# Layer norm inside a window attention's pipeline, weights on GpSimd, and an output stage by whole samples

## The chip, the cores and the metric

The kernel runs on one core of a Trainium2 chip, in one launch. The time is device microseconds of that core, the median of several runs; lower is better. Engines: PE multiplies matrices (PEld is its weight load), DVE is VectorE, ACT is ScalarE, POOL is GpSimd; SP issues most of the DMAs.

## What is computed

The input x has 4 samples of 56 x 56 tokens with 128 channels, float32. Four layers follow each other, each `x = x + layer(group_norm(x))`:

```python
# layer 0: attention in shifted 7x7 windows, then over all tokens, then an MLP
attn_wins = _mha(wins, wq, bq, wk, bk, wv, bv, wo, bo)
xf = xf + _mha(_layernorm(xf, g1, be1), wq, bq, wk, bk, wv, bv, wo, bo)
h = gelu(_layernorm(xf, g2, be2) @ w1 + b1)
xf = xf + (h @ w2 + b2)
# layer 1: edge layer, relu over all pairs of a row, summed
# layer 2: attention whose queries, keys, values and projection are
#   products in the Fourier domain, over the 56 images of a sample
scores = einsum('bhtd,bhsd->bhts', qs, ks) / sqrt(d)
out = einsum('bhts,bhsd->bhtd', softmax(scores), vs)
attention = inorm(fourier(out, wP) + xa)
m = gelu(inorm(fourier(inorm(attention), wM0)) + skip)
m = inorm(fourier(m, wM1)) + skip
output = inorm(m) + attention
# layer 3: convolution over 3 rows, with sums over both axes
g = (agent_sum + time_sum - y) / scale
out = relu(g + res)
```

`inorm` normalizes each image; the group norm has 32 groups of 4 channels.

## The kernel before, in words

Channels lie on the 128 partitions, and a sample is 128 x 3136. Layers 0 and 1 run sample by sample: `fast_windows` (L294), `fast_attention` (L492), the MLP and the edge layer, with about 716 us from one sample to the next. Then come the Fourier layer's stages for all samples together, and last the output stage.

`fast_windows` takes 8 groups of 8 windows (392 tokens). Its loop at the function's end has 12 turns; in each turn a stage of its own works on another group: norm, project, score, value, turn, output. PE, ACT and DVE run in the order in which the code names the instructions (`manual_schedule`); elsewhere a scheduler chooses the order, and then only the engines named in `manual_schedule` keep the code's. The PSUM tag `mm` has four banks.

`fast_attention` begins with a loop over 7 blocks of 448 tokens. In each, PE centres the block (L631), ACT squares it (L633), PE forms the variance (L641), ACT takes the root (L643), DVE the reciprocal (L644), and DVE multiplies the centred block, which lies in PSUM, by it (L520). Two blocks later PE forms queries and keys (L526) and values (L535); ACT moves them out (L527, L537). The normed tokens lie in the ring that later holds the exponentials (L602 writes it, L555 sums it).

The spectra of layer 2 run after the last sample (2910 to 3043 us), `s_pr` being one of their transforms. After them `value_weights` (L1277) loads V, Vrev and P, and DVE makes from them the weights that `attend` loads as `dd`. `attention_weights` (L1334) calls `score_weights` (L1311) on DVE, and then multiplies spectra by these weights: q_u by DVE at L1402, by POOL at L1399, with a product on PE at L1389. `attend` (L1446) uses the result, and `attended_rows` (L1519) turns it into rows and writes them to `yd` in DRAM.

The output stage works on half samples of 28 images. `outputs` (L1958) starts one every 7 turns; in each turn every living half sample does one of its 28 steps, and after the second half of a sample `last_layer` (L1870) follows with its own. All four compute engines keep this written order. A half sample loads a (`xm`) and y (`yd`), and goes back from the Fourier domain with `over_h` (L1665, on PE, seven products with the data as weights) and `over_c` (L1676); ACT scales in between (L1684). It sums squares on PE (L1724) after ACT squared (L1735 takes the root, L1730 adds up). `over_w` (L1692) goes into the Fourier domain, `weighted` (L1707) goes on along the other axis, DVE multiplies by the layer's weights (L1711) and POOL adds the two parts (L1716). This happens for the projection's image, for M0 and for M1. POOL and DVE add images (L1809 to L1861), and DVE takes statistics (L1864), row sums (L1865) and column sums (L1866). `last_layer` folds the group norm into the convolution's weights (`wr`), so that x needs no pass of its own, and the convolution reads x (L1941).

Of the kernel before, what the change touches and what calls it, by code (L numbers as in the profile page):

```python
# [11 lines left out]
F32 = mybir.dt.float32  # L12
# [281 lines left out]
def fast_windows(k, w, xw, xf, mr):  # L294
# [11 lines left out]
    BUFS = 3  # L306
    with ExitStack() as es:
# [20 lines left out]
        scores, values, outs, columns = {}, {}, {}, {}  # L328

        def bank():  # L330
            return psum.tile([P, 512], F32, tag="mm", name="w_mm", bufs=4)
# [65 lines left out]

        norm(0)
        norm(1)
        for n in range(NG + 4):  # L400
            for stage, g in ((norm, n + 2), (project, n), (score, n - 1), (value, n - 2), (turn, n - 3), (output, n - 4)):
                if 0 <= g < NG:
                    stage(g)
# [88 lines left out]
def fast_attention(k, w, xf):  # L492
# [9 lines left out]
    with ExitStack() as es:  # L502
# [3 lines left out]
        va = big.tile([P, 25, P], F32, name="f_va")  # L506

        ring = big.tile([P, RING, NB], F32, name="f_ring")
        h1 = ring[:, 0:NBLK, :].rearrange("p a n -> p (a n)")
        with tc.tile_pool(name="f_ln", bufs=2) as lk, tc.tile_pool(name="f_ps0", bufs=2, space=PSUM) as psum, \  # L510
                tc.manual_schedule(engines={mybir.EngineType.PE}):
            centred, var = {}, {}
            c0 = 0
            for j in range(NBLK + 2):
                if j < NBLK:
                    centred[j] = psum.tile([P, 512], F32, tag="c", name="f_pc")
                    centre(k, lk, centred[j][:, :NB], xf[:, blk(j)], var, j)
                if 0 < j <= NBLK:
                    r = inverse_deviation(k, lk, psum, var.pop(j - 1))
                    nc.vector.tensor_mul(h1[:, blk(j - 1)], centred.pop(j - 1)[:, :NB], r)  # L520
                if j < 2:
                    continue
                b = blk(j - 2)
                for dst, wt, bias in ((qT, w.fq, w.fbq), (kT, w.fk, w.fbk)):
                    pm = psum.tile([P, 512], F32, tag="mm", name="f_pq", bufs=4)
                    nc.tensor.matmul(pm[:, :NB], wt, h1[:, b], start=True, stop=True)  # L526
                    nc.scalar.activation(dst[:, b], pm[:, :NB], AF.Identity, bias=bias)  # L527

                while c0 < 25 and min(c0 * P + 4 * P, TOK) <= b.stop:
                    pm = psum.tile([P, 512], F32, tag="mm", name="f_pv", bufs=4)  # L530
                    n = min(4, 25 - c0)
                    for i in range(n):
                        c = c0 + i
                        for o in half if c == 24 else (slice(0, P),):
                            nc.tensor.matmul(pm[o, i * P:(i + 1) * P], h1[:, c * P:min(c * P + P, TOK)], w.fv,  # L535
                                             start=True, stop=True)
                    nc.scalar.copy(va[:, c0:c0 + n, :].rearrange("p a c -> p (a c)"), pm[:, :n * P])  # L537
                    c0 += 4
        wk = es.enter_context(tc.tile_pool(name="f_wk", bufs=2))
        ps = es.enter_context(tc.tile_pool(name="f_ps", bufs=1, space=PSUM))  # L540
        oT = big.tile([P, TOK], F32, name="f_oT")
# [440 lines left out]
def l2_constants():  # L982
# [44 lines left out]
    c["gw"] = np.concatenate([np.stack([ck * np.cos(a), -ck * np.sin(a)], 1)] * 4)  # L1027
    c["gv"] = np.concatenate([np.stack([ck ** 0.5 * np.cos(a), -ck ** 0.5 * np.sin(a)], 1)] * 4)
# [99 lines left out]
def normed_images(k, w, st, b, pools, x2d, xad, ready):  # L1128
# [16 lines left out]
    nc.gpsimd.memset(xp[:, HH, :], 0.0)  # L1145
# [131 lines left out]
def value_weights(k, I, w, dd):  # L1277


    nc, tc = k.nc, k.tc  # L1280
    with ExitStack() as es:
        wk = es.enter_context(tc.tile_pool(name="d_wk", bufs=1))
        load_weights(k, wk, I, "w2_", w, ("V", "Vrev", "P"))

        half = wk.tile([32, 2, HH], F32, name="d_half")
        nc.vector.tensor_add(half[:, 0, :], w.V[0:32, 0, 0, :], w.Vrev[:, 0, :])
        nc.vector.tensor_sub(half[:, 1, :], w.V[0:32, 1, 0, :], w.Vrev[:, 1, :])
        nc.vector.tensor_scalar_mul(w.V[0:32, :, 0, :], half, 0.5)
        m = wk.tile([P, 8, HH], F32, name="d_m")
        nc.vector.tensor_scalar_add(m, w.V[:, 0], w.pvh[:, 1:2])  # L1290
        d = wk.tile([P, 2, 8, HH], F32, name="d_d")
        t = wk.tile([P, 8, HH], F32, name="d_t")
        nc.vector.tensor_mul(d[:, 0], w.P[:, 0], m)
        nc.vector.tensor_mul(t, w.P[:, 1], w.V[:, 1])
        nc.vector.tensor_sub(d[:, 0], d[:, 0], t)
        nc.vector.tensor_mul(d[:, 1], w.P[:, 1], m)
        t2 = wk.tile([P, 8, HH], F32, name="d_t2")
        nc.vector.tensor_mul(t2, w.P[:, 0], w.V[:, 1])
        nc.vector.tensor_add(d[:, 1], d[:, 1], t2)
        f = wk.tile([P, 3, 8, HH], F32, name="d_f")  # L1300
        for ri in range(2):
            flat = d[:, ri].rearrange("p c r -> p (c r)")
            nc.vector.scalar_tensor_tensor(flat, w.V[:, ri].rearrange("p c r -> p (c r)"), w.pvh[:, 0:1], flat,
                                           ALU.mult, ALU.add)
        nc.scalar.copy(f[:, 0], d[:, 0])
        nc.vector.tensor_sub(f[:, 1], d[:, 1], d[:, 0])
        nc.vector.tensor_add(f[:, 2], d[:, 0], d[:, 1])
        nc.sync.dma_start(dd.rearrange("n g h i x -> (g h i) n x"), f.rearrange("p n c r -> p n (c r)"))


def score_weights(nc, pool, qk, qkr, qks, m, out):  # L1311

    for x in range(2):
        col0 = qk[:, x, :, 0, :]
        nc.vector.tensor_add(col0[:, 0], col0[:, 0], qkr[:, x, 0])
        nc.vector.tensor_sub(col0[:, 1], col0[:, 1], qkr[:, x, 1])
        if x:
            nc.vector.tensor_scalar_mul(col0, col0, m[:, 3:4])  # L1320
        nc.vector.scalar_tensor_tensor(col0[:, 0], qks[:, x], m[:, 2 * x:2 * x + 1], col0[:, 0], ALU.mult, ALU.add)
        if qk.shape[3] > 1:
            s = pool.tile([P, HEADS], F32, tag="s", name="q_skip")
            nc.vector.tensor_scalar_mul(s, qks[:, x], m[:, 1:2])
            rest = qk[:, x, 0, 1:, :]
            nc.vector.tensor_add(rest, rest, bc(s, 1, rest.shape[1]))
    t = pool.tile([P] + list(out.shape[2:]), F32, tag="t", name="q_t")
    for n, (i, op) in enumerate(((1, ALU.add), (0, ALU.subtract))):
        nc.vector.tensor_mul(out[:, n], qk[:, 0, 0], qk[:, 1, n])
        nc.vector.tensor_mul(t, qk[:, 0, 1], qk[:, 1, i])  # L1330
        nc.vector.tensor_tensor(out[:, n], out[:, n], t, op)


def attention_weights(k, I, w, st):  # L1334
# [5 lines left out]
    nc, tc = k.nc, k.tc  # L1340
    with ExitStack() as es:
# [250 lines left out]
CONV_WEIGHTS = ("M0", "M0rev", "M1", "M1rev", "ms", "nb")  # L1592


def conv_weights(k, w, pool, late):

# [527 lines left out]
```

## Time and profile before

| What | us |
|---|---|
| median of 3 runs | 4117.6 |
| lowest and highest run | 4115.57 and 4118.82 |
| profiled execution, its time | 4115.57 |
| profiled execution, its span | 4113.8 |
| windows of sample 1 | 50.7 to 104.5 |
| layer norm and projections of sample 1 | 104.5 to 154.8 |
| spectra of layer 2 | 2910 to 3043 |
| output stage | 3606 to 4114 |

The span runs from the first to the last instruction of the profiled execution; its time has 1.8 us around it. The mean clock granted to PE was 0.929 of full speed. A busy share is a mean over a stretch, and says nothing of what ends a wait. In a row of instructions the mean time of one follows the busy time; "PE n <- ACT m: 20, 7, 5" reads: PE waited 20 us in 7 waits for ACT's m, the longest 5.

### The profile page before, as it was taken

Reading aid. Unit: us, or ns where it says so; the run is one execution under the profiler, and the core shown is the slowest. Engines: PE = TensorE matmul, PEld = TensorE weight load, DVE = VectorE, ACT = ScalarE, POOL = GpSimd, SP = SyncE. Lnnn points to the kernel's source line nnn. Section 1 sums busy time; section 2 is a strip of 40 time slices with the busy share of each in tenths; the row PEclk is TensorE's granted clock in tenths of the full one; section 3 lists DMA queues with packets and bytes.
Section 4 is the critical chain, followed back from the end, with each engine's and each line's share of the span. In section 5 each row is a group of like instructions: output and inputs, shape, how many; then the busy total and the mean of one; then the engine's idle time right before and its main releaser. Section 6 shows DMA issues by size and latency. Waiting matters only on the chain. (4 is left out here: it accounts for less than half of the span.)

```text
span 4113.8 us, 79308 instructions
## 1 busy us (share of the span) xinstructions
PE 3593.8 (87%) x35320; PEld 1623.8 (39%) x35320; DVE 2930.3 (71%) x2659; ACT 2097.6 (51%) x2214; POOL 1145.9 (28%) x596
## 2 busy tenths in 40 slices
PE   6899989989998988999898899989769799877877
PEld 4322234532223453222355322245543333355554
DVE  6688859668885967888586788858658577625443
ACT  4677745567773546777454777745210122133331
POOL 0000018300001820000272000027116489724554
PEclk9999989999998999999899999989779899967777
DMA  2000000000000000000000000000210488330100
GB/s 90 1 1 1 1 16 3 18 1 1 1 1 16 3 18 1 1 1 1 16 3 17 1 1 1 1 1 3 100 65 1 94 174 166 85 110 24 55 16 32
DMA packets 75001, 117.55 MB, mean 29 GB/s; under 512 B 62300, under 2 KB 64092, under 8 KB 69404
## 3 DMA queue, kind: packets, MB, share of 16 engines
q1 hardware_dynamic: 15964, 99.55, 8.1%
q10 hardware_dynamic: 58688, 12.85, 1.9%
q8 instruction: 279, 4.57, 0.5%
q14 instruction: 70, 0.57, 0.0%
HBM read 82.67 MB, written 29.72 MB: 27 GB/s over the span
## 5 line engine op out<-in xcount | busy, mean ns | idle before, releaser
L602 ACT ACTIVATE f_ring<-f_s 128x1792 f32<-128x1792 f32 (+3 forms) x796 | 1098.0, 1430 | 312.8 <-PE f_s L600 310.9
L555 DVE TENSOR_TENSOR f_acc<-f_acc,f_ring 128x1792 f32<-128x1792 f32 x560 | 1134.1, 2025 | 81.8 <-ACT f_ring L602 26.4
L600 PE MATMUL f_s<-f_qT,f_kT 32*128 32x448 f32 x5376 | 738.7, 571 | 56.9 <-ACT f_ring L602 24.1
L844 POOL TENSOR_TENSOR x<-xf,xw 128x343 f32<-128x343 f32 (+2 forms) x36 | 30.0, 834 | 2142.2 <-issue 2069.9
L561 PE MATMUL f_po<-f_ring,f_va 128*32 128x448 f32 x5376 | 589.7, 546 | 0.0
L928 DVE TENSOR_TENSOR e_td<-e_pa,e_c 128x1792 f32<-128x1792 f32 x252 | 491.4, 2016 | 8.0 <-ACT e_a L895 8.0
L930 POOL TENSOR_TENSOR e_tp<-e_a,e_c 128x1792 f32<-128x1792 f32 x140 | 451.7, 3260 | 143.6 <-PE e_acc L935 104.5
L600 PEld LDWEIGHTS f_s<-f_qT,f_kT 32*128 32x128 f32 x5376 | 267.4, 183 | 536.7 <-ACT f_ring L602 366.1
L935 PE MATMUL e_acc<-e_td,t_shared 32*32 32x448 f32 x8064 | 322.2, 545 | 25.9 <-DVE e_td L928 15.3
L932 ACT ACTIVATE e_tp<-e_tp 128x1792 f32<-128x1792 f32 x140 | 235.2, 1697 | 187.3 <-POOL e_tp L930 187.3
L1496 DVE TENSOR_TENSOR u_ud<-u_px,u_d 112x1792 f32<-112x1792 f32 x144 | 240.2, 1708 | 104.6 <-PE u_po L1501 85.9
L561 PEld LDWEIGHTS f_po<-f_ring,f_va 128*32 128x32 f32 x5376 | 132.8, 108 | 398.3 <-issue 397.3
L644 DVE RECIPROCAL n_r<-n_r 128x392 f32<-128x392 f32 (+1 forms) x60 | 163.6, 2749 | 110.3 <-ACT n_r L643 110.1
L1501 PE MATMUL u_po<-u_ud,AT 112*64 112x448 f32 x960 | 202.2, 551 | 35.2 <-DVE u_ud L1496 35.2
L935 PE MATMUL e_acc<-e_tp,t_shared 32*32 32x448 f32 x4480 | 220.4, 544 | 2.4 <-ACT e_tp L932 2.2
L1498 POOL TENSOR_TENSOR u_up<-xh,u_d 112x1792 f32<-112x1792 f32 x64 | 195.2, 3075 | 33.5 <-PE u_po L1501 17.6
L935 PEld LDWEIGHTS e_acc<-e_td,t_shared 32*32 32x32 f32 x8064 | 133.4, 103 | 150.5 <-DVE e_td L928 60.5
L555 DVE TENSOR_TENSOR f_acc<-f_ring 128x1792 f32<-128x1792 f32 x28 | 56.7, 2025 | 115.4 <-ACT f_ring L602 115.4
L1389 PE MATMUL q_acc<-q_u,S 64*64 64x448 f32 x1024 | 104.4, 559 | 30.2 <-DVE q_u L1402 25.4
L1501 PEld LDWEIGHTS u_po<-u_ud,AT 112*64 112x64 f32 x960 | 65.2, 138 | 160.4 <-issue 87.4
L1501 PE MATMUL u_po<-u_up,AT 112*64 112x448 f32 x576 | 126.7, 547 | 0.0
L935 PEld LDWEIGHTS e_acc<-e_tp,t_shared 32*32 32x32 f32 x4480 | 94.1, 103 | 54.6 <-ACT e_tp L932 18.5
(452 smaller groups left out, 4756.8 us busy)
## 6 DMA issues: line engine op xcount, KB each, us to landing
u_d<-dd SPq DMA_DIRECT2D x48, 784.0 KB
xw<-in_x SPq DMA_DIRECT2D x4, 1568.0 KB
x2d<-x SPq DMA_DIRECT2D x4, 1568.0 KB
x_xs<-xad ACTq DMA_DIRECT2D x32, 196.0 KB
xm<-x_ev ACTq DMA_DIRECT2D x64, 98.0 KB
o_a<-xm SPq DMA_DIRECT2D x8, 784.0 KB
o_x<-x2d SPq DMA_DIRECT2D x4, 1568.0 KB
out<-o_o SPq DMA_DIRECT2D x12, 448.0 KB
```

The source lines that it names most:

```text
L555: nc.vector.tensor_add(acc, slots(j, 0) if c == 1 else acc, slots(j, c))
L561: nc.tensor.matmul(po[heads[h], :NB], va[o, c, heads[h]], p, start=(c == 0), stop=(c == 24))
L600: nc.tensor.matmul(ss[:, i, :NB], kT[heads[h], c * P:(c + 1) * P], qT[heads[h], blk(j)], start=True, stop=True)
L602: nc.scalar.activation(ring[:, slot:slot + m, :], ss[:, :m, :NB], AF.Exp, scale=scale)
L644: nc.vector.reciprocal(r, r)
L928: nc.vector.tensor_tensor(t, am, cm, ALU.max)
L930: nc.gpsimd.tensor_sub(t, bc(a.rearrange("p (l n) -> p l n", l=8), 1, 4), cm)
L932: nc.scalar.activation(tf, tf, AF.Relu)
L935: nc.tensor.matmul(acc[quarters[q], r, :NB], k.ident[o, o], t[o, q].rearrange("p l n -> p (l n)"), start=(g == 0), stop=(g == len(EDGE_TUR ...
L1496: nc.vector.tensor_mul(u, bc(px[:, :, :NB], 2, m), dm)
L1498: nc.gpsimd.tensor_mul(u, bc(x, 2, m), dm)
L1501: nc.tensor.matmul(po[64 * b2:64 * b2 + 64, :NB], st.AT[:, 8 * i + h0 + q, 2 * bp + b2, :], u[:, b2, q, :], start=(left == 16), stop=(left ...
```

## The change

Three parts change at once.

1. `fast_windows` is called from `fast_attention` and gets the tiles for queries, keys and values. Four stages join its loop: `central` five groups behind the newest, `variance` six, `divide` ten and `attended` eleven, so that the loop has 19 turns. The blocks are the windows' groups of 392. Four groups share one variance bank, 32 partitions each, and so one root and one reciprocal; `divide` spreads the reciprocal over the partitions by a product on PE. The centred tokens go to SBUF. The tag `mm` has three banks, and the variance the fourth. Values are moved out by DVE, not ACT. The loop over 7 blocks is gone. The ring is allocated after the windows.
2. `value_weights` and `score_weights` use GpSimd where they used DVE (a multiply and an add in place of each `scalar_tensor_tensor`), and are called ahead of `spectra`, with their loads. A memset of the spectra moves from GpSimd to DVE. The pool for the last part of `attention_weights` opens after the softmax's has closed. `attended_rows` writes its rows in another layout (parity, channel, image).
3. `half_sample`, `last_layer` and their written order go. `sample_output` works on whole samples in 17 steps, the next sample starts every 10 turns, and the scheduler chooses the order on every engine. Going back from the Fourier domain is done by `images`: 28 small products and two wide ones for 14 images. Square sums are taken by ACT and DVE. The group norm before the convolution is a pass over the sample (n), with row sums (nl) and column sums (na) of its result.

The core of the diff for parts 1 and 2:

```diff
+def fast_windows(k, w, xw, xf, mr, Q, K, V):
...
+            return psum.tile([P, 512], F32, tag="mm", name="w_mm", bufs=3)
...
+        def central(g):
+            pc = bank()
+            nc.tensor.matmul(pc[:, :N], k.centre, xf[:, group(g)], start=True, stop=True)
+            squares[g] = wk.tile([P, N], F32, name="w_sq")
+            nc.scalar.activation(squares[g], pc[:, :N], AF.Square)
+            nc.vector.tensor_copy(h1[:, group(g)], pc[:, :N])
+        def variance(g):
+            q = g % HALF
+            if q == 0:
+                roots[g // HALF] = psum.tile([P, 512], F32, tag="var", name="w_var", bufs=1)
+            var = roots[g // HALF]
+            nc.tensor.matmul(var[32 * q:32 * q + 32, :N], k.ones_c[:, 0:32], squares.pop(g), start=True, stop=True)
+            if q == HALF - 1:
+                r = wk.tile([P, N], F32, name="w_r")
+                nc.scalar.activation(r, var[:, :N], AF.Sqrt, scale=1024.0, bias=eps)
+                nc.vector.reciprocal(r, r)
+                roots[g // HALF] = r
+        def divide(g):
+            q = g % HALF
+            pr = bank()
+            rows = slice(32 * q, 32 * q + 32)
+            nc.tensor.matmul(pr[:, :N], k.ones[rows, :], roots[g // HALF][rows, :], start=True, stop=True)
+            nc.vector.tensor_mul(h1[:, group(g)], h1[:, group(g)], pr[:, :N])
+        def attended(g):
+            nonlocal chunk
+            b = group(g)
+            for dst, wt, bias in ((Q, w.fq, w.fbq), (K, w.fk, w.fbk)):
+                pm = bank()
+                nc.tensor.matmul(pm[:, :N], wt, h1[:, b], start=True, stop=True)
+                nc.scalar.activation(dst[:, b], pm[:, :N], AF.Identity, bias=bias)
+            while chunk < 25 and (g == NG - 1 or chunk * P + 4 * P <= b.stop):
+                pm = bank()
+                m = min(4, 25 - chunk)
+                for i in range(m):
+                    c = chunk + i
+                    for o in halves if c == 24 else (slice(0, P),):
+                        nc.tensor.matmul(pm[o, i * P:(i + 1) * P], h1[:, c * P:min(c * P + P, TOK)], w.fv,
+                                         start=True, stop=True)
+                nc.vector.tensor_copy(V[:, chunk:chunk + m, :].rearrange("p a c -> p (a c)"), pm[:, :m * P])
+                chunk += m
         norm(0)
         norm(1)
-        for n in range(NG + 4):
-            for stage, g in ((norm, n + 2), (project, n), (score, n - 1), (value, n - 2), (turn, n - 3), (output, n - 4)):
+        for n in range(NG + 11):
+            for stage, g in ((norm, n + 2), (project, n), (score, n - 1), (value, n - 2), (turn, n - 3), (output, n - 4),
+                             (central, n - 5), (variance, n - 6), (attended, n - 11), (divide, n - 10)):
                 if 0 <= g < NG:
                     stage(g)
...
-def fast_attention(k, w, xf):
+def fast_attention(k, w, xw, xf, mr):
...
-        ring = big.tile([P, RING, NB], F32, name="f_ring")
...
-            for j in range(NBLK + 2):
...
+        fast_windows(k, w, xw, xf, mr, qT, kT, va)
+        ring = es.enter_context(tc.tile_pool(name="f_ring", bufs=1)).tile([P, RING, NB], F32, name="f_ring")
...
-        nc.vector.tensor_sub(d[:, 0], d[:, 0], t)
...
+    nc.gpsimd.tensor_sub(d[:, 0], d[:, 0], t)
...
+def all_score_weights(k, I, w, pool, wk, st):
...
+    st.g = pool.tile([P, 2, 16, HEADS], F32, name="q_g")
+    st.g4 = pool.tile([P, 2, 1, HEADS], F32, name="q_g4")
+    load_weights(k, wk, I, "w2_", w, ("qk", "qkr", "qk4"))
+    score_weights(nc, wk, w.qk, w.qkr, w.qks, k.qm, st.g)
+    score_weights(nc, wk, w.qk4[:, :, 0].rearrange("p x r (c h) -> p x r c h", c=1), w.qk4[:, :, 1], w.qks, k.qm4,
+                  st.g4)
+    nc.gpsimd.tensor_scalar_mul(st.g4[:, 1], st.g4[:, 1], k.qm4[:, 4:5])
...
+        wks.close()
+        big = es.enter_context(tc.tile_pool(name="q_end", bufs=1))
...
+                with tc.tile_pool(name="g_wk", bufs=1, side="right") as wk:
+                    all_score_weights(k, I, w2, sp, wk, st)
+                    value_weights(k, I, w2, wk, dd)
+                    spectra(k, w2, st, x2d, xad)
                 x1s.close()
-                value_weights(k, I, w2, dd)
...
```

The other lines of the two weight functions change like the one shown. The new output stage:

```python
def sample_output(k, w, st, b, pools, x2d, xm, yd, out):
...
    def images(y, mat):
        for j in range(4):
            pv = bank()
            for i in range(7):
                for q in range(2):
                    for ri in range(2):
                        o = 64 * q + 32 * ri
                        nc.tensor.matmul(pv[o:o + 32, i * HH:(i + 1) * HH], y[:, q, :, 7 * j + i], k.gh[:, ri, :],
                                         start=True, stop=True)
            v = wk.tile([P, 7 * HH], F32, tag="v", name="o_v")
            nc.scalar.copy(v, pv[:, :7 * HH])
            pd = banks()
            for q in range(2):
                o = slice(64 * q, 64 * q + 64)
                nc.tensor.matmul(pd[:, q, :7 * HH], mat[o], v[o], start=True, stop=True)
            yield j, slice(14 * j, 14 * j + 14), pd[:, :, :7 * HH].rearrange("p q (t h) -> p q t h", t=7)
    def spectrum(src):
        z = big.tile([P, 2, 32, 28], F32, tag="z", name="o_z")
...
    def weighted(z, m, dc=None):
        y = big.tile([112, 2, 32, 28], F32, tag="y", name="o_y", bufs=3)
        s2 = wk.tile([112, 2, 2, 28], F32, tag="s2y", name="o_s2y")
        for i in range(2):
            cs = slice(16 * i, 16 * i + 16)
            ts = []
            for x in range(2):
                pd = banks()
                for ri in range(2):
                    for q in range(2):
                        o = slice(64 * q, 64 * q + HH)
                        nc.tensor.matmul(pd[:112, q, :NB], k.fv[o, x, ri, :], z[o, ri, cs, :].rearrange("p c t -> p (c t)"),
                                         start=(ri == 0), stop=(ri == 1))
                t = wk.tile([112, 2, 16, 28], F32, tag="t%d" % x, name="o_t")
                p4 = pd[:112, :, :NB].rearrange("p q (c t) -> p q c t", c=16)
                nc.vector.tensor_mul(t, p4, bc(bc(m[:, x, cs], 1, 2), 3, 28))
                if dc is not None and i == 0 and x == 0:
                    nc.vector.tensor_scalar_mul(dc, pd[0:1, :, 0:28], w.nms[0:1])
                ts.append(t)
            nc.gpsimd.tensor_add(y[:, :, cs, :], ts[0], ts[1])
            nc.scalar.activation(ts[1], y[:, :, cs, :], AF.Square)
            nc.vector.tensor_reduce(s2[:, i], ts[1].rearrange("p q c t -> p q t c"), AX.X, ALU.add)
        ps = bank()
        for i in range(2):
            nc.tensor.matmul(by_parity(ps[:, :HH]), k.ones[:112, :], s2[:, i], start=(i == 0), stop=(i == 1))
        return y, ps[:, :HH]
...
    x = big.tile([P, HH, HH], F32, tag="x", name="o_x")
    nc.sync.dma_start(x, x2d[b])
    a = big.tile([P, HH + 2, HH], F32, tag="a", name="o_a")
    a0 = a[:, 0:HH, :]
    nc.sync.dma_start(a0, xm[b])
    y = big.tile([112, 2, 32, 28], F32, tag="y", name="o_yh", bufs=3)
    nc.sync.dma_start(y, yd[b])
    nc.vector.tensor_copy(y[0:1, :, 0, :], st.dc[:, b])
    yield
    att = big.tile([P, HH, 64], F32, tag="t", name="o_att")
    nc.gpsimd.memset(att[:, :, HH:], 0.0)
    att_ = att[:, :, :HH]
    s2 = wk.tile([P, HH], F32, tag="s2", name="o_s2")
    for j, ts, pd in images(y, k.gw):
        nc.vector.tensor_add(by_parity(att_[:, ts]), by_parity(a0[:, ts]), pd)
        square_sums(s2, j, att_[:, ts])
        if j == 1:
            yield
    var = wk.tile([P, HH], F32, tag="var", name="o_var")
    nc.vector.tensor_copy(var, over_w(s2))
    yield
    f1 = factor(var, w.ng[:, 1:2], "f1")
    f2 = wk.tile([P, HH], F32, tag="f2", name="o_f2")
    nc.vector.tensor_mul(f2, f1, f1)
    nc.vector.tensor_mul(f2, f2, var)
    f2 = factor(f2, w.ng[:, 2:3], "f2")
    nc.vector.tensor_mul(f2, f2, f1)
    z = spectrum(att)
    yield
    y, var = weighted(z, w.M0)
    fs = wk.tile([P, HH], F32, tag="fs", name="o_fs")
    nc.vector.tensor_scalar_mul(fs, f2, w.ms[:, 0:1])
    nc.vector.tensor_mul(a0, att_, bc(fs, 2, HH))
    yield
    f3 = wk.tile([P, HH], F32, tag="f3", name="o_f3")
    nc.vector.tensor_mul(f3, f2, f2)
    nc.vector.tensor_mul(f3, f3, var)
    f3 = factor(f3, w.ng[:, 3:4], "f3")
    nc.vector.tensor_mul(f3, f3, f2)
    scale(y, f3)
    nc.gpsimd.tensor_mul(att_, att_, bc(f1, 2, HH))
    nc.gpsimd.tensor_add(x, x, att_)
    yield
    g = big.tile([P, HH, 64], F32, tag="t", name="o_g")
    nc.gpsimd.memset(g[:, :, HH:], 0.0)
    g_ = g[:, :, :HH]
    for j, ts, pd in images(y, k.gv):
        nc.vector.tensor_add(by_parity(a0[:, ts]), by_parity(a0[:, ts]), pd)
        nc.scalar.activation(g_[:, ts], a0[:, ts], AF.Gelu, bias=w.bg)
        if j == 1:
            yield
    yield
    z = spectrum(g)
    yield
    dc = wk.tile([1, 2, 28], F32, tag="dc", name="o_dc")
    y, var = weighted(z, w.M1, dc)
    yield
    f4 = factor(var, w.ng[:, 4:5], "f4")
    scale(y, f4)
    nc.vector.tensor_copy(y[0:1, :, 0, :], dc)
    yield
    s2 = wk.tile([P, HH], F32, tag="s2", name="o_s3")
    for j, ts, pd in images(y, k.gv):
        for q in range(2):
            nc.vector.scalar_tensor_tensor(by_parity(a0[:, ts])[:, q], by_parity(g_[:, ts])[:, q], w.ms[:, 2:3], pd[:, q],
                                           ALU.mult, ALU.add)
        square_sums(s2, j, a0[:, ts])
        if j == 1:
            yield
    f5 = factor(over_w(s2), w.ng[:, 5:6], "f5")
    yield
    gs = wk.tile([P, NBLK, 6], F32, tag="gs", name="o_gs")
    for j in range(NBLK):
        tj = a0[:, 8 * j:8 * j + 8, :]
        nc.gpsimd.tensor_mul(tj, tj, bc(f5[:, 8 * j:8 * j + 8], 2, HH))
        nc.vector.scalar_tensor_tensor(flat(x)[:, blk(j)], flat(a0)[:, blk(j)], w.bo, flat(x)[:, blk(j)], ALU.add, ALU.add)
        nc.vector.bn_stats(gs[:, j, :], flat(x)[:, blk(j)])
    yield
    mr = group_norm_factors(k, wk, bank, gs)
    nc.vector.tensor_mul(mr[:, 0:1], mr[:, 0:1], mr[:, 1:2])
    nc.vector.tensor_scalar_mul(mr[:, 0:1], mr[:, 0:1], -1.0)
    nc.gpsimd.memset(a[:, 0, :], 0.0)
    nc.gpsimd.memset(a[:, HH + 1, :], 0.0)
    n = a[:, 1:HH + 1, :]
    nc.scalar.activation(n, x, AF.Identity, bias=mr[:, 0:1], scale=mr[:, 1:2])
    nl = wk.tile([P, HH + 2], F32, tag="nl", name="o_nl")
    nc.vector.tensor_reduce(nl, a, AX.X, ALU.add)
    na = wk.tile([P, 3, HH], F32, tag="na", name="o_na")
    nc.vector.tensor_reduce(na[:, 1, :], n.rearrange("p l a -> p a l"), AX.X, ALU.add)
    nc.vector.tensor_sub(na[:, 0, :], na[:, 1, :], n[:, HH - 1, :])
    nc.vector.tensor_sub(na[:, 2, :], na[:, 1, :], n[:, 0, :])
    ps = bank()
    for t in range(3):
        nc.tensor.matmul(ps[:, 0:HH], w.W[:, t, :], nl[:, t:t + HH], start=(t == 0), stop=(t == 2))
    for t in range(3):
        nc.tensor.matmul(ps[:, HH:2 * HH], w.W[:, t, :], na[:, t, :], start=(t == 0), stop=(t == 2))
    s12 = wk.tile([P, 2, HH], F32, tag="s12", name="o_s12")
    nc.vector.tensor_scalar_add(s12[:, 0, :], ps[:, 0:HH], w.bs)
    nc.vector.tensor_copy(s12[:, 1, :], ps[:, HH:2 * HH])
    o = big.tile([P, HH, HH], F32, tag="t", name="o_o")
    nc.gpsimd.tensor_add(o, bc(s12[:, 0, :], 2, HH), bc(s12[:, 1, :], 1, HH))
    yield
    for j0 in range(0, NBLK, 2):
        m = min(2, NBLK - j0)
        pd = banks()
        for i in range(m):
            for t in range(3):
                at = (j0 + i) * NB + t * HH
                nc.tensor.matmul(pd[:, i, :NB], w.Wr[:, t, :], flat(a)[:, at:at + NB], start=(t == 0), stop=(t == 2))
        js = slice(j0 * NB, (j0 + m) * NB)
        oj = flat(o)[:, js]
        o2 = oj.rearrange("p (i x) -> p i x", i=m)
        nc.vector.tensor_add(o2, o2, pd[:, :m, :NB])
        nc.scalar.activation(oj, oj, AF.Relu)
        nc.gpsimd.tensor_add(oj, oj, flat(x)[:, js])
        nc.sync.dma_start(out[b].rearrange("p l a -> p (l a)")[:, js], oj)
        if j0 == 2:
            yield
    yield
...
def outputs(k, w, st, x2d, xm, yd, out):
    tc = k.tc
    with ExitStack() as es:
        pools = [es.enter_context(tc.tile_pool(name=n, bufs=2)) for n in ("o_big", "o_wk")]
        pools.append(es.enter_context(tc.tile_pool(name="o_ps", bufs=2, space=PSUM)))
        samples = [sample_output(k, w, st, b, pools, x2d, xm, yd, out) for b in range(B)]
        turn, live = 0, []
        while samples or live:
            if samples and turn % 10 == 0:
                live.append(samples.pop(0))
            live = [g for g in live if next(g, 0) is None]
            turn += 1
```

## The prediction

> **What bounds the kernel now.** I read the engine totals first, then the busy table by stage, and in each of the three stages that the change touches the waits, the rows and the order of time.
>
> ```profile
> span 4113.8 us, 79308 instructions
> PE 3593.8 (87%) x35320; PEld 1623.8 (39%) x35320; DVE 2930.3 (71%) x2659; ACT 2097.6 (51%) x2214; POOL 1145.9 (28%) x596
> ```
>
> PE's 87% is an average. The stages (PE busy; DVE; ACT; POOL; clock granted to PE; DMA share; GB/s):
>
> ```profile
> 50.70:104.50 53.80, 50.64 (x593) 36.51 (x593) 35.37 (x76) 32.09 (x53) 8.60 (x21) 0.96 0.01 2
> 104.50:154.80 50.30, 34.51 (x108) 18.56 (x108) 25.04 (x14) 22.09 (x36) 0.00 (x0) 0.86 0.00 0
> ...
> 3055.00:3072.00 17.00, 0.00 (x0) 0.00 (x0) 13.40 (x28) 1.83 (x5) 8.30 (x5) 0.50 0.39 124
> 3600.00:3700.00 100.00, 74.70 (x418) 54.50 (x419) 29.37 (x44) 33.92 (x61) 26.72 (x17) 0.68 0.31 113
> ...
> 3900.00:4000.00 100.00, 86.31 (x488) 56.53 (x487) 45.83 (x82) 29.35 (x52) 47.24 (x25) 0.81 0.04 17
> ```
>
> Row 1, windows of sample 1: PE is full. Row 2, layer norm and projections: PE is a third idle on a partly halved clock. Row 3: PE does nothing, DVE makes weights. Rows 4 and 5, output stage: no engine is full, so chains and PE's clock set it. In row 2 the waits read:
>
> ```profile
> DVE n_r L644 <- ACT n_r L643: 22.4, 7, 5.4
> ACT n_sq L633 <- PE f_pc L631: 18.2, 7, 5.8
> PE f_pc L631 <- DVE f_ring L520: 13.5, 5, 5.4
> ```
>
> This is a ring: centre, square, variance, root, reciprocal (2953 ns, seven times), multiply, next centre. In row 3 DVE's order of time shows when the attention weights can begin:
>
> ```profile
> 3041.51 0.62 DVE L225 COPY xh<-s_px 112x448 f32<-112x448 f32 x1 [0.95 <-PE s_px L1243]
> ...
> 3052.76 0.62 DVE L1307 TENSOR_TENSOR d_f<-d_d 128x448 f32<-128x448 f32 x1
> ...
> 3071.43 2.02 DVE L1402 TENSOR_TENSOR q_u<-q_px,q_g 128x1792 f32<-128x1792 f32 x1
> ```
>
> The last copy of the spectra ends at 3042, the first product q_u starts 29 us later. In the output stage the waits are long and spread over all engines, which is how a pipeline of chains looks:
>
> ```profile
> POOL o_y L1716 <- DVE o_t L1711: 194.8, 14, 28.8
> DVE o_s L1730 <- PE o_b L1724: 89.6, 16, 13.0
> ACT o_z L1696 <- PE o_d L1692: 67.4, 14, 10.2
> PE o_d L1676 <- ACT o_v L1684: 37.1, 5, 10.2
> ```
>
> The first half sample's copy L1764 starts at 3613.1, the eighth's at 3936.6: 46.2 us per half, 92.4 per sample, and 177 from there to the end at 4114.
>
> **What the Trainium skill says.** "TensorE: Matmul & The Clock Gate", What's actually happening: PE runs at half clock after an idle window of about 3.4 us and at full clock only after a busy one. The trace agrees: the output stage's slices show .68 to .81. "GPSIMD Engine Reference", 3.1 Elementwise: an fp32 tensor_tensor takes 1.96 times VectorE's time. Here the same 128x1792 form takes 3260 ns on POOL (L930) and 2016 on DVE (L928), 1.62 times; I use that. "ScalarE: Activation LUTs", What ACT_TABLE_LOAD costs: 1283 ns, plus a drain of 1380. The trace has 1283 and shows no drain.
>
> **A. Layer norm inside the windows.** Removed per sample: the 50.3 us loop. Added: its work as four stages of the windows' loop, which grows from 12 turns to 19. A steady turn of the windows takes PE 5.85 us (2220.22 to 2226.07). The stages add, for the groups that fall in turns 0 to 11: seven centres and six variances at .66 us (pitch of the 392-column pairs), one block of projections 2.1, two divides .66: 12. Giving one of four banks to the variance I put at 1. The one root and reciprocal per four groups (.6 + 1.28 table + 2.75) is waited for twice; two other turns' work covers part, so 2.5 + 1.8 stay. Turns 12 to 18 hold the rest of PE's work, 17, and a wait of .7 per turn, since divide, DVE's multiply and the projections follow each other with little else to run: 22 to 26. V's copies go from ACT to DVE (.54 x 7), where PE's next turn hides them; uncovered they are 3.8 per sample. Sum: 54 + 12 + 2.5 + 26, less overlap at the seam, is 92 to 93, against 102 for both stages now (53 + 49). That is 8 to 10 per sample, -34 for four. Ends: PE's own work at full clock, 50 + 27 of projections and norm + 8 of fill, would save 16 per sample (-64); three banks and the ping-pong could eat all (0); a loss is left out, since turns 12 to 18 would have to take over 4.8 us each, twice PE's work in them.
>
> **B. Layer 2's weights on GpSimd.** DVE's value weights (3045 to 3053) and score weights (to 3071.3) leave DVE; about 55 POOL instructions, 20 us on DVE now (6.7 + 13.4 in the two stretches from 3044), 33 at 1.62 times, some 40 with the small ones at their floor, run at the start of the spectra (2910 to 3043), where POOL has 1.14 us of work in 138: they are hidden, and stay so while POOL needs under 130. Their loads stand ahead of one image load on SP's queue; about 1 MB at 400 GB/s is 2.5 us, behind work of the earlier images. The memset of one row goes to DVE, .3, beside PE's transforms. What is late next: PE's fold of the spectra, its copies, then two POOL q_sc, so the first q_u comes at 3053, not 3071.4: -18.5. Against that, the folding matrix can be loaded only when the softmax is over, +2. I take -17; ends -22 and -10 (if loads of the attention's other inputs last end at 3061).
>
> **C. Output stage by whole samples.** Removed: eight half samples 46 us apart, up to five alive, on a written order. Added: four samples, the next starting when ten of seventeen steps are done. Row prices: an image block is 28 small matmuls (spectra's s_pr: 112 in 6.73 us, .060 each; cold 12.16, .109) and two wide ones, 3.3 us; DVE's add .97 (L1819); gelu .95; a spectrum 2 x 3.3 (L1692); weighted 2 x 3.26 on PE (L1707), then multiply 1.09, POOL 2.12 (L1716), square .95, strided sum 1.8, matmul .85, root with table 1.6, reciprocal and gain .7, scaling 2.02: 20 with the hand-overs. Period, in PE's order:
> - second images, gelu, spectrum: 13.2 + 1 + 6.6 = 21
> - weighted M1, factor, scaling, PE mostly idle: 20
> - third images and the next sample's first: 26.4 + two waits for square sums of 5.5 = 38
> - next spectrum with the wait for its copies: 10
> - POOL's multiply, statistics, factors, the normalization pass on ACT (3.1): 8
> - on DVE the contiguous row sum 3.65 and the strided 6.0 (L1865, L1866 for half the size: 1.77, 3.02), before the next weighted's multiplies: 14
> - POOL's o (5.9) and the two passes over att, ahead of the scaling: 15
>
> That is 126, against 92.4. PE idles over 3.4 us in five of these pieces and comes back cold; a cold image block costs 1.4 to 2 more, so I take 130 (bounds 113, if the last two overlap, and 145, if images stay cold throughout: 12 x 1.7 = 20). Lead: x, a and y, 4 MB against 1.2 MB ahead of the first work, +6; first images 18.7, spectrum 10, weighted 20, factor and scaling 5, cold start 5: second images start at 3677, 64 after 3613. Tail after the last start: 21 + 20 + 19 + 8 + 10 + 10 + 3 + 7 + 12, 110. The later loads wait on SP's queue for the buffers and the last outputs of the sample two before, which ends about 50 us ahead of the need; uncovered, 10 us each. The attended rows keep their transposes and copies in another layout, at no cost beside a DMA that the stage waits for anyway (28.6 for yd); dearer writes could add 5. Stage: 64 + 3 x 130 + 110 = 564 against 501: +63 (P = 126: +51).
>
> Sum: -34 - 17 + 63 = +12 on a span of 4113.8, with 1.8 around it the profiled execution's 4115.6. The median of the runs shown, 4117.6, is 2 above; so 4130.
>
> **The rivals.**
> - R1, the output's period stays short. Place: the third images' overlap with the next sample and the two last pieces of the period. POOL is busy under half of the time and DVE too, so nothing forbids that these hide. Price: 3 us per us of period. From P = 123 the whole is faster by over 0.2%; at 113 it gives 4117.6 - 51 + 12 = 4079. Against: PE's waits in before already reach 10 us with five alive, and only two are alive now.
> - R2, the norm hides wholly under PE's windows: -64 - 17 + 63 = -18, 4100. For: DVE and ACT have 18 to 22 us free in row 1. Against: seven turns have no windows to run.
> - R3, images stay cold: P = 142, +36: 4166. For: clock .68 in row 4.
> - R4, A yields nothing (its added waits in place of the removed): 4164.
> - B is hidden anyway by the loads (-10): 4137, inside the forecast's case.
>
> **How the numbers follow.** Forecast .44 (4110 to 4155), R1 .20, R2 .12, R3 .14, R4 .10. This kernel's measurement can tell 0.2%, 8 us, from no change. Faster: R1 .19, R2 .09, forecast's edge .02: .30. Same: forecast .14, R1 .01, R2 .03: .18. Slower: .52. The range 4085 to 4185 leaves out R1's lower half, some .10, and .06 above for R3 with R4. The forecast's own range is 4110 to 4155.
>
> **What would show it.** A right: windows and norm of a sample together 90 to 95 us, four reciprocals' waits gone from DVE but two per sample of 2 to 3 us on PE. B right: first q_u 9 to 12 us after the last xh copy. C right: starts of the gelu blocks 126 to 133 us apart, PE's clock below .75 there, the longest PE waits at scaling and spectrum. Wrong, if that distance is under 120 or over 140, or if norm and windows take 85 or 101.

## The result, and the profile after

The changed kernel takes 4163.91 us (median of 4 runs, 4160.94 to 4167.04) against 4118.21 before in the same comparison: ratio 1.0109, 95% interval 1.0091 to 1.0126, so 46 us slower. The profiled execution has a span of 4159.2. The forecast was 4130, slower, so +12 where +46 was measured; its own case was 4110 to 4155, and 4085 to 4185 was the range with the rivals.

The engine totals of the changed kernel hardly differ from those of before:

```profile
span 4159.2 us, 82693 instructions
PE 3573.2 (86%) x37112; PEld 1599.7 (38%) x37112; DVE 3008.2 (72%) x2657; ACT 2047.0 (49%) x2073; POOL 1127.3 (27%) x616
```

The change is seen only by stage. The rows below are of the changed kernel, with the columns of the earlier table: turns 0 to 11 of sample 4's windows (all turns in which a window stage works), turns 12 to 18, the spectra, and two stretches of the output stage.

```profile
2184.70:2254.00 69.30, 65.29 (x626) 41.73 (x626) 40.72 (x84) 38.39 (x64) 6.92 (x18) 0.93 0.05 22
2254.00:2282.30 28.30, 24.12 (x99) 13.57 (x98) 10.70 (x15) 9.30 (x16) 0.00 (x0) 1.00 0.00 1
2905.00:3036.40 131.40, 94.47 (x1232) 83.81 (x1232) 76.26 (x307) 33.73 (x76) 33.47 (x50) 0.72 0.29 109
3680.00:3780.00 100.00, 60.45 (x627) 39.40 (x624) 70.35 (x76) 22.22 (x31) 31.73 (x15) 0.69 0.00 1
3880.00:3980.00 100.00, 64.68 (x778) 38.69 (x774) 60.65 (x59) 28.68 (x38) 30.91 (x14) 0.81 0.17 57
```

The tail of the windows' loop, turns 12 to 18, is 28 us, of which PE is busy 24. In the output stage PE's busy time per 100 us was 75 and 86 in the rows shown of before and is 60 and 65 here; DVE's was 29 and 46 and is 70 and 61.

Between fixed points of the two profiled executions (us, each measured in its own trace):

| Distance | before | after | change |
|---|---|---|---|
| start to the last exponential of sample 4 | 2663.3 | 2652.3 | -11.0 |
| from there to the last product of the spectra | 379.0 | 384.0 | +5.0 |
| to the first product with q_u | 31.2 | 16.8 | -14.4 |
| to the last copy of the attended rows | 526.2 | 526.6 | +0.5 |
| to the end | 514.1 | 579.4 | +65.3 |

So layer norm gave 11 where 34 was forecast, the weights 9 where 17 was, and the output stage cost 65 where 63 was. The rows sum to 45, against 46 in the medians.

### The profile page after: what moved, and what is told of

Its sections match the earlier page's. It is cut to its first block, busy times and chain, and to the rows that moved or that the text cites. A ratio compares the mean times of both kernels' runs of the same rounds, so it can differ in the third digit from the quotient of the medians.

```text
span 4159.2 us, 82693 instructions
## 1 busy us (share of the span) xinstructions
PE 3573.2 (86%) x37112; PEld 1599.7 (38%) x37112; DVE 3008.2 (72%) x2657; ACT 2047.0 (49%) x2073; POOL 1127.3 (27%) x616
## 5 line engine op out<-in xcount | busy, mean ns | idle before, releaser
L594 PEld LDWEIGHTS f_po<-f_ring,f_va 128*32 128x32 f32 x5376 | 132.9, 109 | 398.9 <-issue 397.9
L1540 POOL TENSOR_TENSOR u_up<-xh,u_d 112x1792 f32<-112x1792 f32 x64 | 193.3, 3045 | 50.5 <-issue 21.5
L1543 PEld LDWEIGHTS u_po<-u_ud,AT 112*64 112x64 f32 x960 | 65.3, 138 | 160.6 <-issue 87.9
L1429 PE MATMUL q_acc<-q_u,S 64*64 64x448 f32 x1024 | 102.5, 556 | 16.7 <-DVE q_u L1442 12.7
L1439 POOL TENSOR_TENSOR q_u<-iS,q_g 128x1792 f32<-128x1792 f32 x24 | 77.5, 3268 | 124.0 <-PE s_px L1276 92.5
```

The source lines that it names most:

```text
L594: nc.tensor.matmul(po[heads[h], :NB], va[o, c, heads[h]], p, start=(c == 0), stop=(c == 24))
L1429: nc.tensor.matmul(acc[halves[hb % 2], 2 * i + hb // 2, :NB], x[o], u[o, 8 * hb:8 * hb + 8, :].rearrange("p h t -> p (h t)"), start=start, ...
L1540: nc.gpsimd.tensor_mul(u, bc(x, 2, m), dm)
L1543: nc.tensor.matmul(po[64 * b2:64 * b2 + 64, :NB], st.AT[:, 8 * i + h0 + q, 2 * bp + b2, :], u[:, b2, q, :], start=(left == 16), stop=(left ...
```

## The experiments

A run is told by its ratio to the kernel before, measured on the same chip, since medians of before vary between comparisons (4116.6 to 4119.5).

**The three parts alone, and two together.** The edits are the parts of the diff above, each with what it needs.

> Only the layer norm's stages join the windows' loop; weights and output stage are as before. Theory from the two traces (the tail turns cost 4 us each, so a sample saves 2.5 to 4.5): 4107, which is -11, and -2.5 to -4.5 per sample from the first window product to the first exponential. Rival, the prediction's size of -34 with the loss made somewhere else in the changed kernel: 4084.

Measured: 4101.99, ratio 0.9958 (0.9944 to 0.9972), 15 us less. First window product to first exponential: 99.8 to 101.6 per sample, against 103.2 to 105.9.

> Only layer 2's weights go to GpSimd ahead of the spectra. Theory from the traces (the spectra grow by 5, the first product comes 14 earlier): -8 to -9, so 4109. Rival, the prediction's -17: 4101.

Measured: 4106.6, ratio 0.9970 (0.9958 to 0.9982), 11 less.

> Only the output stage by whole samples. Theory from the traces: +65, so 4183, with 132 from gelu to gelu of two samples. Rival, the three parts hinder each other and the stage alone costs less: under 4165.

Measured: 4184.22, ratio 1.0164 (1.0149 to 1.0179), 67 more; gelu to gelu 133.1, 135.6, 132.9.

> Layer norm's stages and the weights on GpSimd, with the output stage by half samples as before. Theory, the parts add: -20, so 4098. Rival, the prediction's sizes: -51, so 4067.

Measured: 4093.59, ratio 0.9945 (0.9931 to 0.9959), 24 less. The parts add: -15 - 11 + 67 is +41 against 46 for the changed kernel, with intervals of about 6 on each. The loss is the output stage's, and the two other parts are gains, together half as large as forecast (24 of 51).

**What holds the output stage: DVE's waits for POOL.** The changed kernel's order of time on DVE and POOL at the group norm ahead of the convolution, in the first sample (start, length; the PE row is the one that waits):

```profile
3744.23 5.45 POOL L1809 TENSOR_TENSOR o_att<-o_att,o_f 128x3136 f32<-128x3136 f32 x1 [17.80 <-PE o_b L1729]
...
3744.65 5.05 DVE L1901 TENSOR_TENSOR gf_t<-gf_mv,gf_mr 128x1 f32<-128x1 f32 x1
3749.73 0.16 DVE L1902 TENSOR_TENSOR gf_t<-gf_t 128x1 f32<-128x1 f32 x1
3749.76 6.79 POOL L1810 TENSOR_TENSOR o_x<-o_x,o_att 128x3136 f32<-128x3136 f32 x1
3750.81 5.75 DVE L1903 TENSOR_TENSOR gf_t<-gf_t,gf_mv 128x1 f32<-128x1 f32 x1
...
3756.71 0.56 PE L1905 MATMUL o_b<-gf_t,t_shared 128*128 128x1 f32 x2 [7.34 <-DVE gf_t L1903]
```

A subtraction of one element per partition takes 5.05 us: it ends when POOL's instruction on the next sample's images ends. The addition (L1903), two steps on in this chain, takes 5.75 and ends when POOL's next instruction ends. In the last sample, after which no other follows, each takes 0.16. The Trainium skill, "GPSIMD Engine Reference", 1. Specifications, says that POOL's SBUF interfaces are shared with VectorE and that they contend with DVE's instructions that have two SBUF inputs or a two-port mode; it gives no size. The trace agrees and gives one: 5.05 and 5.75 us beside POOL, 0.16 without. The test writes the same factors with per-partition scalars, so that each instruction has one tensor input (the product of mean and reciprocal root behind them is rewritten in the same way):

```diff
-    nc.vector.tensor_sub(t, mv[:, 0:1], mr[:, 0:1])
-    nc.vector.tensor_mul(t, t, t)
-    nc.vector.tensor_add(t, t, mv[:, 1:2])
+    nc.vector.tensor_scalar(t, mv[:, 0:1], mr[:, 0:1], None, ALU.subtract)
+    nc.vector.tensor_scalar(t, t, t, mv[:, 1:2], ALU.mult, ALU.add)
```

> The changed kernel, with the factors of the last group norm formed by instructions of one tensor input and per-partition scalars, in place of the two-input ones that took 5.05 and 5.75 us in three samples. Theory, DVE's two-input instructions wait for POOL's long ones over the memory port and the wait is on the path: three times 10 to 11 less, -30, so 4134. Rival, DVE would wait there anyway for the pieces behind it: within 6 of 4164.

Measured: 4135.16, ratio 1.0038 (1.0023 to 1.0052) against 1.0109 (1.0091 to 1.0126) for the changed kernel, 29 less. In the first sample both instructions now run beside one of POOL's that lasts as long as before, and over the four samples they stay as short (last two rows: shortest, median, longest in ns):

```profile
3748.48 5.45 POOL L1809 TENSOR_TENSOR o_att<-o_att,o_f 128x3136 f32<-128x3136 f32 x1 [17.80 <-PE o_b L1729]
3748.90 0.21 DVE L1855 TENSOR_SCALAR gf_t<-gf_mv,gf_mr 128x1 f32<-128x1 f32 x1
3753.19 0.27 DVE L1856 TENSOR_SCALAR gf_t<-gf_t,gf_mv 128x1 f32<-128x1 f32 x1
...
L1855 DVE TENSOR_SCALAR gf_t<-gf_mv,gf_mr x4: 211/214/214, 3748.9 to 4106.2; 128x1 f32<-128x1 f32 x4
L1856 DVE TENSOR_SCALAR gf_t<-gf_t,gf_mv x4: 266/268/273, 3753.2 to 4106.5; 128x1 f32<-128x1 f32 x4
```

Gelu to gelu is 123.8, 124.6 and 127.0, where the changed kernel has 132.0, 132.7 and 132.2. That is 21.5 in three periods, and the whole stage of the profiled execution is 22 shorter (557.0 against 579.4). The medians differ by 29, with some 9 to either side; the profiled executions are the fastest of the changed kernel's runs and the slowest of this one's. So of the 10.8 that DVE was held in each period, 7 (traces) to 10 (medians) lay on the path, and 10 to 11 was expected. Without these waits the stage is still 43 longer than before (514.1) in the traces.

**What else: the number of chains alive.** The kernel before, with one digit changed:

```diff
-            if waiting and turn % 7 == 0:
+            if waiting and turn % 14 == 0:
```

> The kernel before, with a half sample started every 14 turns, not 7, so that two or three are alive in place of up to five, as in the changed kernel, all else kept. Theory, the number alive sets how much of each chain is hidden: a turn falls from 6.6 only to 4.4 or so, 62 per half sample in place of 46, so 4117 + 7 x 16 = 4229. Rival, the work of an engine sets it, and a turn with half the work takes half the time: 4115 to 4140.

Measured: 4233.01, ratio 1.0285 (1.0264 to 1.0305), 116 more. The eight starts (L1764) now lie between 3614.8 and 4087.7, 67.6 apart instead of 46.2:

```profile
L1764 ACT COPY o_y<-dc x8: 219/222/237, 3614.8 to 4087.7; 1x28 f32<-1x28 f32 x8
```

A turn fell only from 6.6 to 4.8 us with half the work in it. The first theory holds and the rival is out: with two or three chains alive, latencies stay open that four or five cover. The run shows this for half samples in a written order; that it explains all of the changed kernel's remaining 43 is argued from it, not shown, since whole samples also differ in their instructions.

The changed kernel with a small shift of the overlap:

```diff
-            if samples and turn % 10 == 0:
+            if samples and turn % 9 == 0:
```

> The changed kernel with the next sample started every 9 turns, not 10: its first images then stand one step earlier against the sample before. If PE's idle stretch at the second weighting is what the next sample could fill, the distance from gelu to gelu falls from 132 by 5 to 15, so 4120 to 4150. If the chain of one sample alone sets the distance, or the queues only change places, within 8 of 4164.

Measured: 4156.58, ratio 1.0089 (1.0069 to 1.0108), 8 less with overlapping intervals: inconclusive. Gelu to gelu was 123.1 once and 129.9 and 129.5 after that, but the stretch from the last gelu to the end grew from 97.4 to 103.8.

**Where layer norm's gain went: the tail.** PE's rows of the changed kernel in two turns of the tail (the rows for the values, L454, are left out):

```profile
2266.53 0.92 PE L437 MATMUL w_mm<-w_r,c_ones 32*128 32x392 f32 x2
...
2268.20 0.90 PE L445 MATMUL w_mm<-w_h,w_fq 128*128 128x392 f32 x2 [0.75 <-DVE w_h L438]
2268.93 0.82 PE L445 MATMUL w_mm<-w_h,w_fk 128*128 128x392 f32 x2
...
2269.68 0.92 PE L437 MATMUL w_mm<-w_r,c_ones 32*128 32x392 f32 x2
...
2271.35 0.90 PE L445 MATMUL w_mm<-w_h,w_fq 128*128 128x392 f32 x2 [0.75 <-DVE w_h L438]
```

A turn with values is 4.04 us, without them 3.15. Divide (L437) is followed by a wait of 0.75 for DVE's multiply, then by the products that need it. Of the seven turns in sample 4's tail, the last five have such a wait, 1.15 once and 0.75 four times: 4.2 in all. In the two before them the last centre and variances stand between. The test puts one turn more between them:

```diff
-        for n in range(NG + 11):
+        for n in range(NG + 12):
-... (attended, n - 11), (divide, n - 10)):
+... (attended, n - 12), (divide, n - 10)):
```

> Norm and weights with the output stage as before, and the projections one turn later, so that PE has a divide between a divide and the projections that need it. Theory, the tail's turns lose .75 each to that hand-over: about -5 per sample, -20 in all, so 4073 where norm and weights gave 4094. Rival, PE's own work and the added turn bind: within 6 of 4094.

Measured: 4081.18, ratio 0.9905 (0.9889 to 0.9922) against 0.9945, 16 less: 4 per sample, the size of the waits, where 5 was expected. A turn with values is 3.26 here, with no wait:

```profile
2261.72 0.92 PE L437 MATMUL w_mm<-w_r,c_ones 32*128 32x392 f32 x2
2262.57 0.93 PE L445 MATMUL w_mm<-w_h,w_fq 128*128 128x392 f32 x2
2263.33 0.82 PE L445 MATMUL w_mm<-w_h,w_fk 128*128 128x392 f32 x2
2263.99 1.05 PE L454 MATMUL w_mm<-w_fv,w_h 128*128 128x128 f32 x8
2264.98 0.92 PE L437 MATMUL w_mm<-w_r,c_ones 32*128 32x392 f32 x2
```

**Where the weights' gain went: POOL's order.** The run of norm and weights, after the spectra:

```profile
3031.54 9.49 POOL L1439 TENSOR_TENSOR q_u<-iS,q_g 128x1792 f32<-128x1792 f32 x3 [92.65 <-PE s_px L1276]
...
3040.99 6.62 POOL L1415 TENSOR_TENSOR q_sc<-q_g,q_ww 128x896 f32<-128x896 f32 x4
3042.71 0.20 ACT L1414 COPY q_g<-q_pg 128x56 f32<-128x56 f32 x1 [8.06 <-POOL q_sc L1415]
...
3046.16 3.96 DVE L1442 TENSOR_TENSOR q_u<-q_px,q_g 128x1792 f32<-128x1792 f32 x2 [14.49 <-ACT q_px L1421]
```

With the weights ready early, POOL begins three q_u at once, and q_sc stands behind them. ACT's small copies have two buffers, so the third waits for q_sc, and behind it on ACT wait the copies that DVE's first q_u needs.

```diff
-                    g0 = wk.tile([P, HH], F32, name="q_g0")
+                    g0 = wk.tile([P, HH], F32, name="q_g0", bufs=4)
```

> Norm and weights with the output stage as before, and four buffers in place of two for the small copies that POOL's q_sc reads, so that ACT goes on to the large copies without POOL. Theory, the first product waits for POOL's three q_u ahead of q_sc: -6 to -7, so 4087. Rival, something else ends last there: within 3 of 4094.

Measured: 4087.76, ratio 0.9920 (0.9904 to 0.9936) against 0.9945, 10 less with overlapping intervals. The trace shows the mechanism and 6.8 of the gain: from the last product of the spectra to the first with q_u are 10.1 us, where norm and weights had 16.9. DVE now waits 7.64 ahead of its first q_u, not 14.49.

> Norm and weights with the output stage as before, the projections one turn later and four buffers for the small copies. Theory, both gains add since they lie in different stages: 4118 - 24 - 16 - 10 = 4068. Rival, the copies' gain of 10 was partly scatter (its trace shows 7): 4074.

Measured: 4074.28, ratio 0.9900 (0.9883 to 0.9916), 42 less than before: the fastest version, which beats both kernels. Its interval, 4068 to 4082, holds both the sum and the rival's 4074, so these are not told apart.

**Why the spectra grew by 5.** The changed kernel at the statistics of the next sample; before, the same instruction (L1162) took 0.22:

```profile
2935.64 2.95 DVE L1195 SCALAR_TENSOR_TENSOR s_sq<-s_d,s_sq 128x56 f32<-128x56 f32 x1
2935.75 0.24 POOL L1363 TENSOR_TENSOR q_g<-q_g,q_t 128x32 f32<-128x32 f32 x1
2935.96 1.12 POOL L1330 TENSOR_TENSOR d_d<-d_d,d_t 128x448 f32<-128x448 f32 x1
...
2937.39 1.12 POOL L1334 TENSOR_TENSOR d_d<-d_d,d_t 128x448 f32<-128x448 f32 x1
...
2939.71 0.37 PE L1204 MATMUL s_pt<-s_t,t_shared 128*128 128x1 f32 x1 [4.04 <-DVE s_t L1203]
```

DVE is held through a row of POOL's instructions, and PE waits 4.04. The delay goes with the weights: the first inverse transform (`s_px`) comes 287.7 to 289.3 us after the last exponential in the ten runs that have the weights on POOL, the changed kernel among them, and 283.2 to 283.8 in the four that do not. A rival is the loads of the weights, which now stand ahead of the next sample's image. It is out for this stretch: from the first sample's first product to the end of the next sample's statistics reads (L1182, before L1149) there are 16.7 us in every one of the fourteen. From there to the inverse transform the kernel before takes 3.8 and the changed one 6.9, and the held instruction stands there; 1.0 more lies ahead of the first product.

Two runs move DVE's operands to PSUM and write the group norm's factors with scalars, on top of the fastest version (the second also copies `half[4]` and `half[5]` to PSUM first):

```diff
-    nc.vector.tensor_mul(d, d, d)
+    nc.vector.tensor_copy(dp, d)
+    nc.vector.tensor_mul(dp, d, dp)
...
-    nc.vector.scalar_tensor_tensor(sq, d, HH / 4, sq, ALU.mult, ALU.add)
+    nc.vector.scalar_tensor_tensor(sq, dp, HH / 4, sq, ALU.mult, ALU.add)
```

> The same, and the per-image statistics ahead of the spectra in a form in which no arithmetic instruction of DVE on the path but one reads two SBUF tensors (one operand in PSUM, or scalars). Theory, POOL's two-input weights hold up DVE there: the first inverse transform of the spectra, which came 4 us late with the weights on POOL, comes at its old distance, and the whole is 4 to 5 less than without it: 4064. Rival, the delay is from the order of the loads: no change.

Measured: 4078.01, ratio 0.9907 (0.9892 to 0.9922), no gain. The wait had moved to the sum of two SBUF tensors that was left, which now took 3.02, while the one with a PSUM operand took 0.22.

> As the run with one operand in PSUM, whose wait moved to the one instruction left that reads two SBUF tensors (3.02 us); here that one is gone too. Theory, POOL's two-input instructions hold DVE's up: no statistics instruction of DVE takes over .7 there, the first inverse transform comes at 285 us after the last exponential, not 289, and the whole is 4070. Rival, some other wait of 4 us takes its place: 289 again, and 4074 to 4078.

Measured: 4077.36, ratio 0.9898 (0.9880 to 0.9915), no gain. None of the rewritten instructions of this sample's statistics takes over 0.27 there any more and PE's wait there is 2.52, yet the first inverse transform comes at 288.6. The time reappears elsewhere: the first sample's products start 3.2 later than in the fastest version (266.6 against 263.4, and 264.2 to 265.5 in the other runs with the weights on POOL), behind the added copies and behind scalings that are slower beside POOL as well (1.59 for one of 128x56 that took 0.25 before). The scaling of the next whole sample takes 2.46, against 1.91 before. So POOL's hold on DVE is shown, instruction by instruction; that it is the whole of the 5 us is not, and the repair by rewriting single instructions failed.

## Why the prediction was right in sign and short in size

- **C, the output stage.** Right in sum: +63 forecast, +65 in the traces, +67 alone. From gelu to gelu 132 against 130. The first sample's second images start 57 after its first work, and the first loads are waited for 8 longer: together 65 against 64. The tail behind the last sample's second images took 104 against 110. But two errors met inside the 130: the sum of pieces, 126, had DVE's waits for POOL at nothing, and 4 were added for a cold PE. That the period came within 2 is in part luck. In the first period of the trace, cut where PE begins the next piece (3658.1, 3675.6, 3696.3, 3731.9, 3744.6, 3790.8), the list's first four pieces took 17.5, 20.8, 35.6 and 12.6, against 21, 20, 38 and 10. The last three together took 46.3 against 37, and the 10.8 in which DVE was held stand among them. Without those waits the period is 124 to 127, so the pieces came out right, and no run measured the cold addend by itself. R1 is out, since a faster kernel needed a period of 123 or less, and so is R3, which needed 142.
- **A, layer norm.** The mechanism was right, and one term was mis-sized: "Turns 12 to 18 hold the rest of PE's work, 17, and a wait of .7 per turn ... 22 to 26". Measured: 28.2 in each sample, in sample 4 with PE busy 24.1 of them and waiting 4.2. The hand-over, 0.75, was right, though five turns have it and not seven. PE's work was not. By the prediction's own prices these turns hold one centre, two variances, seven blocks of projections and six divides, which is 20.6; 17 is the sum without the divides. The other 3.5 is pitch: in the rows of the later run above it is .85, .76, .66 and .99, where .66 was taken for the 392-column pairs; why it differs is not shown. Turns 0 to 11 took 69.3 to 70.0 against 68.5, and the 2 taken off for overlap at the seam did not come. So windows and norm of a sample together take 97.5 to 98.3 us, outside the 90 to 95 that were named as the sign of a right forecast, and a sample saved 2.5 to 4.5 in the profiled executions, not 8 to 10.
- **B, the weights.** The step that failed is "two POOL q_sc, so the first q_u comes at 3053": 11 us after the spectra, measured 16.8, because three q_u stand ahead of q_sc on POOL. That queue was named and not checked for what the early weights set free. "They are hidden" failed too: the spectra take 5 more with the weights in them. POOL's instructions hold up DVE's there, which is shown for single ones and not for the whole 5. The early loads are 2.1 MB, not "about 1 MB", though the next sample's statistics did not wait for them. The late folding matrix cost 2.1, as forecast.
- **The total.** 4164 lies above the forecast's own 4110 to 4155. By number it is R4's and near R3's, but neither happened: A gave a third (traces) to nearly half (alone) of its gain. The sign came from C; of the 33 that the traces' sum lies above the forecast's, A's shortfall is 23 and B's 8.

## What to carry to other kernels

Work moved to an idle GpSimd is not free because GpSimd is idle: look for DVE's short instructions with two SBUF inputs on a chain beside it, and give them per-partition scalars or a PSUM operand. Here that freed instructions of one element, and was worth 22 to 29 us. Around the spectra it gained nothing: scalings with scalars on 128x56 and 128x3136 were slower beside POOL too (1.59 and 2.46 us against 0.25 and 1.91). Keeping POOL's long instruction out of such a stretch was not tried. When stages are fused into a software pipeline, price the turns after the main work has run out by themselves, in order, on the engine that issues them, and put one turn between a hand-over and its user. When fewer and larger pieces replace many small ones, count the chains alive at once: here starting half samples half as often, with half the work in a turn, stretched the distance from 46.2 to 67.6 us.

## What the runs showed of the hardware that was not expected

A DVE tensor_tensor on 128x1 took 5.05 and 5.75 us beside POOL instructions of 5.45 and 6.79, and 0.16 alone; the same sum with scalars took 0.21 and 0.27 beside them. POOL's L1809 took 5.45 beside them and 5.45 at its first call, where none of them ran, so the holding goes one way there; POOL had begun first each time, and no run shows the other order.

Not every POOL instruction holds them. Near 2939 us of the changed kernel two DVE instructions of the same 128x1 form and with two tensor inputs (L1201, L1203) lie within a POOL tensor_scalar (L1333, 2938.60 to 2940.03), which has one tensor input, and took 0.42 and 0.16; eight runs show this, with 0.16 to 0.42. The POOL instructions that ended as a held DVE instruction ended (L1809, L1810, L1334) are tensor_tensors with two.
